# Seven block products instead of eight for the second half of batch 6, with the two-batch products two tiles sooner

## Chip, cores and metric

The kernel runs on one core of a Trainium2 chip. The metric is the device time of one execution in microseconds (us). Before the change the median of three runs is 302.89 us (302.75 to 303.0).

The engines are called as in the profile: PE is TensorE's matmuls, PEld its weight loads, DVE VectorE, ACT ScalarE, POOL GpSimd, SP SyncE. ACT, POOL and SP also issue DMAs.

## What is computed

There are 8 batches of 1024 tokens with 512 features, all in float32. Each batch has its own 512 x 512 matrix, made from the batch's condition vector:

```python
# cond: layernorm, two dense layers with an exact GELU -> x_a, x_b, each [8, 512, 8]
layer = base_layer[None] + einsum('bdr,bkr->bdk', x_a, x_b)
x = x + (x + einsum('btc,bco->bto', x, layer))          # first layer and residuals
ys = cond / sqrt(512)
d = rsqrt(einsum('bi,io->bo', ys * ys, weight * weight) + 1e-8)
out = x + einsum('bsi,io->bso', x * ys[:, None, :], weight) * d[:, None, :]
```

Both layers and all residual additions are linear in x. So for each batch `out[b] = x[b] @ M[b]` with `M[b] = (2 I + layer) (I + diag(ys) weight diag(d))`.

## The kernel before, in words

The matrices `M[b]` are made on the chip (tiles `q`), and then x is multiplied by them. Float32 values are split for PE into a rounded part and the rest, both of the type float32r. A product a r is taken as three matmuls: high by high, high by low, low by high.

The work on x is the main loop. `main(b, t)` computes 128 tokens by 512 outputs: 4 chunks of the contraction by three matmuls of 128x512, 12 in all, into one bank of PSUM (pool `po`, four banks). ACT copies it to SBUF and issues the store. `load_x` loads half a batch (SP), and `split_x` splits 256 tokens of it (a cast on ACT, a subtract on DVE). `split_p` splits `q[b]` into `ph[b]` and `pl[b]`. The lists in `after` say which other steps are emitted behind which tile; `place(i)` turns the running number i of a tile into batch and tile.

The matrices of batches 4 and 5, and of 6 and 7, are made two at a time by `Pair`, with seven block products for each pair of batches. One `unit` of it (six matmuls of 128x512, 14 units in all) is emitted behind each tile from the number `first` on. `early` and `prepare` make its right-hand sides on DVE and ACT, and `rank_term` adds the rank-8 part (four matmuls, four adds on DVE).

Batch 7 is not done by `main`. `Seven` multiplies it with Strassen's scheme in Winograd's form: the batch's x and the matrix are cut into 2 x 2 blocks, and seven block products take the place of eight. `make_right` forms four sums of blocks of `q[7]` on DVE, casts them on ACT and subtracts on DVE for the rest; it also splits the three blocks that are used as they are. `make_left(g)` does the same with sums of blocks of x, for a quarter of the tokens of each half of the batch. `part(g)` then runs the seven products. Each is 12 matmuls of 128x256, 6 for each of two groups of 128 tokens. They go in the order 1, 5, 6, 2, 7, 3, 4 into three banks: `w` takes products 1, 6, 7 and 4, each added onto the one before it, `z` takes 5 and 3, and `v` takes 2. After each product the bank is copied by ACT (1, 5, 6, 4) or added by DVE (2, 7, 3) into the output tiles `o1` and `o2`. So a product of bank w has to wait until the evacuation of the one before it has read the bank. `part` stores `o1` behind product 3 and `o2` behind product 4. In the last part product 4 is copied and stored for each 128 tokens by itself, out of one bank.

Matmuls keep the order of the program text. On DVE and ACT the steps of the main loop and of `Seven` are not held to it: the compiler that lays out the program fixes the order, and then each engine works its queue in order. Tiles of a tag share as many buffers as `bufs` says. `late_pools` closes the pools from which the matrices were made, and the tiles of `Seven` (`tl`, `th`, `sums`, `sl`, `sh`, `x22`, `o2`) then use their memory. `q`, the loaded x, `xs` and `xa` are in pool `big`, nine buffers.

Of the kernel before, what the change touches and what calls it, by code (L numbers as in the profile page):

```python
# [30 lines left out]
def cond_resid_kernel(ctx: ExitStack, tc: tile.TileContext, small, cond, condrows, consts,  # L31
# [12 lines left out]
    def mm(*args, **kw):  # L44
        tc.keep_in_program_order(nc.tensor.matmul(*args, **kw))  # L45
# [601 lines left out]
    def p_tiles(b):  # L647
        ph[b] = ppool.tile([P, KC, D], F32R, tag="ph", name=f"ph_{b}")
        pl[b] = ppool.tile([P, KC, D], F32R, tag="pl", name=f"pl_{b}")
# [173 lines left out]
    class Seven:  # L823
# [5 lines left out]

        ORDER = (1, 5, 6, 2, 7, 3, 4)

        def __init__(self, b):
            self.b, self.left = b, {}

        def make_right(self):
            b, late = self.b, pools["late"]
            t = late.tile([P, 4, 2, HD], F32R, tag="tl", name=f"tl_{b}", bufs=1)  # L840
            h = late.tile([P, 4, 2, HD], F32R, tag="th", name=f"th_{b}", bufs=1)
            raws = late.tile([P, 4, 2, HD], F32, tag="sums", name=f"traw_{b}", bufs=2)
            t1, t2, t3, t4 = (raws[:, i] for i in range(4))
            b11, b12 = q[b][:, 0:2, 0:HD], q[b][:, 0:2, HD:D]
            b21, b22 = q[b][:, 2:4, 0:HD], q[b][:, 2:4, HD:D]
            p_tiles(b)
            for rows, cols in ((slice(0, 4), slice(0, HD)), (slice(2, 4), slice(HD, D))):
                nc.scalar.copy(ph[b][:, rows, cols], q[b][:, rows, cols])
                nc.vector.tensor_sub(pl[b][:, rows, cols], q[b][:, rows, cols],
                                     ph[b][:, rows, cols].bitcast(F32))  # L850
            for o, x, y in ((t1, b12, b11), (t2, b22, t1), (t3, b22, b12), (t4, b21, t2)):
                nc.vector.tensor_sub(o, x, y)
            for i in range(0, 4, 2):
                at = slice(i, i + 2)
                nc.scalar.copy(h[:, at], raws[:, at])
                nc.vector.tensor_sub(t[:, at], raws[:, at], h[:, at].bitcast(F32))
            self.right = {5: (h[:, 0], t[:, 0]), 6: (h[:, 1], t[:, 1]), 7: (h[:, 2], t[:, 2]),
                          4: (h[:, 3], t[:, 3])}
            for p, rows, cols in ((1, slice(0, 2), slice(0, HD)), (2, slice(2, 4), slice(0, HD)),
                                  (3, slice(2, 4), slice(HD, D))):  # L860
                self.right[p] = ph[b][:, rows, cols], pl[b][:, rows, cols]

        def make_left(self, g):
            b, late = self.b, pools["late"]
            at = slice(2 * P * g, 2 * P * (g + 1))
            top, low = raw[b, 0][:, :, at], raw[b, 1][:, :, at]
            a11, a12, a21, a22 = top[:, 0:2], top[:, 2:4], low[:, 0:2], low[:, 2:4]
            s = late.tile([P, 4, 2, 2 * P], F32R, tag="sl", name=f"sl_{b}_{g}", bufs=2)
            h = late.tile([P, 4, 2, 2 * P], F32R, tag="sh", name=f"sh_{b}_{g}", bufs=2)
            x = late.tile([P, 2, 2, 2 * P], F32R, tag="x22", name=f"x22_{b}_{g}", bufs=2)  # L870
            xa = big.tile([P, 2, KC, 2 * P], F32R, tag="big", name=f"xa_{b}_{g}")
            nc.scalar.copy(xa[:, 0], top)
            nc.vector.tensor_sub(xa[:, 1], top, xa[:, 0].bitcast(F32))
            raws = late.tile([P, 4, 2, 2 * P], F32, tag="sums", name=f"sraw_{b}_{g}", bufs=2)
            s1, s2, s3, s4 = (raws[:, i] for i in range(4))
            nc.vector.tensor_add(s1, a21, a22)
            nc.vector.tensor_sub(s2, s1, a11)
            for i, (o, u, v) in enumerate(((s3, a11, a21), (s4, a12, s2))):
                nc.vector.tensor_sub(o, u, v)
            for i in range(0, 4, 2):  # L880
                two = slice(i, i + 2)
                nc.scalar.copy(h[:, two], raws[:, two])
                nc.vector.tensor_sub(s[:, two], raws[:, two], h[:, two].bitcast(F32))
            nc.scalar.copy(x[:, 0], a22)
            nc.vector.tensor_sub(x[:, 1], a22, x[:, 0].bitcast(F32))
            self.left[g] = {5: (h[:, 0], s[:, 0]), 6: (h[:, 1], s[:, 1]), 7: (h[:, 2], s[:, 2]),
                            3: (h[:, 3], s[:, 3]), 4: (x[:, 0], x[:, 1]),
                            1: (xa[:, 0, 0:2], xa[:, 1, 0:2]), 2: (xa[:, 0, 2:4], xa[:, 1, 2:4])}

        def product(self, g, p, bank, m, first):  # L890
            (lh, ll), (rh, rl) = self.left[g][p], self.right[p]
            for kk in range(2):
                for i, (a, r) in enumerate(((lh, rh), (lh, rl), (ll, rh))):
                    mm(bank[:, m, :], a[:, kk, m * P:(m + 1) * P], r[:, kk, :],
                       start=(first and m == 0 and kk == 0 and i == 0),
                       stop=(kk == 1 and i == 2), skip_group_check=True)

        def part(self, g, last):
            b, bank = self.b, {}
            o1, o2 = (pools["late"].tile([P, 2, D], F32, tag="o2", name=f"o{i}_{b}_{g}", bufs=3)  # L900
                      for i in range(2))
            for p in self.ORDER:
                key = {5: "z", 3: "z", 2: "v"}.get(p, "w")
                first = p in (1, 5, 2)
                if first:
                    pool, tag = (acc, "acc") if key == "v" else (po, "po")
                    bank[key] = pool.tile([P, 2, HD], F32, tag=tag, name=f"s{key}_{b}_{g}")
                u = bank[key]
                for m in range(2):
                    self.product(g, p, u, m, first)  # L910
                    if p == 4 and last:
                        nc.scalar.copy(o2[:, m, 0:HD], u[:, m])
                        self.store(o2, g, 1, slice(m, m + 1))
                if p == 1:
                    nc.scalar.copy(o1[:, :, 0:HD], u)
                elif p == 5:
                    nc.scalar.copy(o2[:, :, HD:D], u)
                elif p == 6:
                    nc.scalar.copy(o1[:, :, HD:D], u)
                elif p == 2:  # L920
                    nc.vector.tensor_add(o1[:, :, 0:HD], u, o1[:, :, 0:HD])
                elif p == 7:
                    nc.vector.tensor_add(o2[:, :, HD:D], u, o2[:, :, HD:D])
                elif p == 3:
                    nc.vector.tensor_add(o1[:, :, HD:D], u, o1[:, :, HD:D])
                    self.store(o1, g, 0, slice(0, 2))
                elif not last:
                    nc.scalar.copy(o2[:, :, 0:HD], u)
                    self.store(o2, g, 1, slice(0, 2))

        def store(self, o, g, half, ms):
            at = half * HT + 2 * P * g
            nc.scalar.dma_start(
                out[self.b, at + P * ms.start:at + P * ms.stop, :].rearrange("(m p) d -> p m d", p=P),
                o[:, ms, :])
# [16 lines left out]
    place = lambda i: divmod(i, NTT)  # L952
    for b in range(1, 4):
        first = (b - 1) * NTT
        at(*place(max(0, 4 * b - 8)), load_rank, b)
        at(*place(4 * b - 2), rank_term, b)
        for j in range(2):
            at(*place(first + 3 + j), split_p, b, j)
    for b, first in ((4, 13), (6, 30)):

        at(*place(first - 9), load_d, b)
        at(*place(first - 6), new_pair, b)
# [9 lines left out]
        at(*place(first + 15), split_p, b, 0)  # L972
        at(*place(first + 16), split_p, b, 1)
        if b == 4:
            at(*place(first + 19), split_p, b + 1, 0)
            at(*place(first + 21), split_p, b + 1, 1)
    seven = Seven(NB - 1)
    at(*place(46), late_pools)
    at(*place(47), seven.make_right)
    at(*place(49), load_x, NB - 1, 0)  # L980
    at(*place(50), load_x, NB - 1, 1)
    at(*place(52), seven.make_left, 0)
    at(*place(54), seven.make_left, 1)

    for b in range(NB - 1):
        for t in range(NTT):
            if t == 0 and b + 2 < NB:
                p_tiles(b + 1)
            main(b, t)
            i = b * NTT + t  # L990
            if t % 4 == 0 and i + 4 < (NB - 1) * NTT:
                load_x(*divmod(i // 4 + 1, NHALF))
            if t % 2 == 0 and i + 4 < (NB - 1) * NTT:
                split_x(*divmod(i // 2 + 2, NTT // 2))
            for f, args in after.get((b, t), ()):
                f(*args)
    for g in range(2):
        seven.part(g, g == 1)


# [67 lines left out]
```

## Time and profile before

| | us |
|---|---|
| median of three runs | 302.89 |
| the profiled execution's own time | 302.81 |
| its span, from the first to the last instruction | 301.0 |
| PE busy | 294.3 |
| DVE busy | 194.0 |
| ACT busy | 150.2 |

The granted clock of TensorE is 1.000 as the mean of the span. The first 80 us make the matrices of batches 0 to 3. From 80.7 on the main loop runs, and from 276.5 on the two parts of batch 7. The profile comes from one execution. "Busy" is time in which at least one instruction of the engine ran. Matmuls overlap one another, so the distance of their starts tells their price, not their duration. In a timeline a bracket gives the idle time of the engine before the instruction and what ended it. The chain of waits goes back from the last instruction to what released each one.

### The profile page before, as it was taken

The page shows a single profiled execution, that of the slowest core. Times are in us where ns is not written, and L with a number is a line of the kernel's source. Part 1 is how long each engine was busy: PE and PEld are TensorE (multiplying, and loading weights), DVE is VectorE, ACT ScalarE, POOL GpSimd, SP SyncE. Part 2 cuts the span into 40 slices and gives each one's busy share as a digit, 9 for nine tenths or more (in the row PEclk, how much of TensorE's full clock was granted, in tenths as well). Part 3 has the DMA queues.
Part 4 walks back from the last instruction along what each step waited for, and adds up shares of the span by engine and source line. Part 5 has one row for each costly group of instructions (what it writes and reads, how often), then busy time and mean ns, then how long its engine had stood idle before and what let it go on. Part 6 is the DMA issues. An engine that isn't in the chain of part 4 may idle for free.

```text
span 301.0 us, 3809 instructions
## 1 busy us (share of the span) xinstructions
PE 294.3 (98%) x1429; PEld 224.8 (75%) x1429; DVE 194.0 (64%) x287; ACT 150.2 (50%) x218; POOL 34.8 (12%) x74
## 2 busy tenths in 40 slices
PE   7999999999999999999999999999999999999994
PEld 2655465466878778888888877888888877888993
DVE  4779750979569889794157549994356238994201
ACT  4756132256566672572457535664465436855130
POOL 0011000057104505100000018000000000000000
PEclk9999999999999999999999999999999999999999
DMA  6999999696519888186124347725144364432033
GB/s 207 412 426 418 407 423 416 216 327 182 197 70 312 320 250 273 72 244 210 69 89 193 87 192 188 233 82 199 50 194 152 128 209 140 165 117 93 12 143 139
DMA packets 19027, 62.12 MB, mean 206 GB/s; under 512 B 2736, under 2 KB 2992, under 8 KB 14656
## 3 DMA queue, kind: packets, MB, share of 16 engines
q1 hardware_dynamic: 6064, 38.78, 34.6%
q10 hardware_dynamic: 9168, 16.78, 15.0%
q0 software_dynamic: 3776, 6.31, 7.7%
q8 instruction: 11, 0.18, 0.2%
q14 instruction: 8, 0.07, 0.1%
HBM read 44.02 MB, written 17.84 MB: 206 GB/s over the span
## 4 chain that ended last, share of the span: by engine, by line
PE 86%; DMA 5%; DVE 5%; ACT 2%; issue 1%; SPq 0%; ACTq 0%
PE po L45 51%; PE pp L45 13%; PE pq L45 7%; PE sw L45 4%; DMA w<-in_w 4%; PE px L45 3%; PE pg L45 2%; PE sz L45 2%; DVE n L62 2%; DMA b_raw<-in_baseT 2%; PE pr L45 1%; PE sv L45 1%; PE pt_t L45 1%; ACT work L62 1%; DVE scr L62 0%
## 5 line engine op out<-in xcount | busy, mean ns | idle before, releaser
L45 PE MATMUL po<-ph,xs 128*128 128x512 f32 x448 | 144.9, 391 | 0.0
L45 PEld LDWEIGHTS po<-ph,xs 128*128 128x128 f32 x448 | 84.1, 188 | 19.3 <-issue 1.7
L45 PE MATMUL po<-pl,xs 128*128 128x512 f32 x224 | 87.3, 390 | 0.0
L62 ACT COPY o<-po 128x512 f32<-128x512 f32 x56 | 32.8, 586 | 60.8 <-PE po L45 60.8
L45 PEld LDWEIGHTS po<-pl,xs 128*128 128x128 f32 x224 | 42.1, 188 | 8.6
L62 DVE TENSOR_TENSOR xs<-x,xs 128x1024 fp32r<-128x1024 f32 x28 | 34.0, 1220 | 10.5 <-ACT xs L62 10.5
L62 DVE TENSOR_TENSOR nl_p<-n,nh_p 128x1024 fp32r<-128x1024 f32 x14 | 17.1, 1222 | 23.1 <-ACT nh_p L62 23.0
L62 ACT CAST xs<-x 128x1024 fp32r<-128x1024 f32 x28 | 29.1, 1052 | 1.2 <-DMA x<-in_x 1.0
L62 DVE TENSOR_TENSOR q<-pr,q 128x512 f32<-128x512 f32 x32 | 20.1, 684 | 13.6 <-PE pr L45 13.6
L511 POOL DMA_DIRECT2D fa<-kept_a x28 | 13.7, 506 | 77.9 <-PE pr L45 77.2
L45 PE MATMUL pq<-nh,bh 128*128 128x512 f32 x48 | 19.8, 412 | 0.0
L45 PE MATMUL pq<-nl,bh 128*128 128x512 f32 x48 | 19.1, 398 | 0.1
L62 ACT COPY q<-pp 128x512 f32<-128x512 f32 x20 | 11.7, 587 | 14.9 <-PE pp L45 14.1
L45 PE MATMUL pq<-nh,bl 128*128 128x512 f32 x48 | 18.9, 394 | 0.0
L62 DVE SCALAR_TENSOR_TENSOR n<-w_sb,ysT,d 128x512 f32<-128x512 f32 x24 | 17.7, 746 | 1.5 <-DMA d<-d_out 1.5
L62 DVE TENSOR_TENSOR pl<-q,ph 128x1024 fp32r<-128x1024 f32 x14 | 16.9, 1220 | 0.1
L62 ACT CAST nh_p<-n 128x1024 fp32r<-128x1024 f32 x14 | 14.7, 1052 | 3.5 <-DVE n L62 1.9
L62 ACT CAST ph<-q 128x1024 fp32r<-128x1024 f32 x14 | 14.6, 1053 | 3.4 <-DVE q L62 3.1
L45 PE MATMUL px<-w,hT 128*32 128x512 f32 x128 | 16.0, 601 | 0.1
L45 PEld LDWEIGHTS pq<-nh,bh 128*128 128x128 f32 x48 | 9.0, 188 | 8.4 <-issue 5.0
L511 POOL DMA_DIRECT2D ft<-kept_t x28 | 13.8, 512 | 4.9 <-DMA kept_t<-st_t 4.9
L62 ACT CAST nh<-n 128x512 fp32r<-128x512 f32 (+1 forms) x10 | 6.9, 707 | 11.5 <-DVE n L62 11.5
(193 smaller groups left out, 407.1 us busy)
## 6 DMA issues: line engine op xcount, KB each, us to landing
w<-in_w SPq DMA_DIRECT2D x16, 1024.0 KB, 10.7
x<-in_x SPq DMA_DIRECT2D x16, 1024.0 KB, 5.3
out<-o ACTq DMA_DIRECT2D x58, 256.0 KB, 2.1
ft<-kept_t POOLq DMA_DIRECT2D x28, 64.0 KB, 3.4
fa<-kept_a POOLq DMA_DIRECT2D x28, 64.0 KB, 3.2
d<-d_out POOLq DMA_DIRECT2D x6, 256.0 KB, 3.9
out<-o ACTq DMA_DIRECT2D x3, 512.0 KB, 2.9
w_sb<-in_weight SPq DMA_DIRECT2D x2, 512.0 KB, 5.3
```

Source lines behind the costliest of these rows:

```text
L45: tc.keep_in_program_order(nc.tensor.matmul(*args, **kw))
L62: return lambda *a, **kw: pin(f(*a, **kw)) if InOrder.on else f(*a, **kw)
L511: nc.gpsimd.dma_start(fold[name, b][32 * c:32 * c + 32, :], kept[name, g][32 * i:32 * i + 32, :])
```

## The change

- `Seven` now takes a batch by halves: part g has the g-th 512 tokens, `make_left(g)` the sums of that half.
- The second half of batch 6 is done by `Seven` too. The main loop ends after 52 tiles instead of 56, and three parts follow: batch 6's second half, then batch 7's two halves. `make_left(1)` of batch 7 is emitted between the first two of these.
- For batch 6 `make_right` has `whole` true and leaves out the split, since `ph[6]` and `pl[6]` exist already. `tl` and `th` get two buffers, `sums` one instead of two.
- Both pairs start two tiles sooner, with their rank terms; the rank terms of batches 2 and 3 move up too, the split of batch 5 goes one tile later, and `late_pools` moves from behind tile 46 to behind tile 44.
- Bank w moves from pool `po` to `acc`. In the last part it is two banks, one for each 128 tokens; each of its evacuations is then two narrower ones, and product 4 runs through before it is copied in the text.

```diff
-        def make_right(self):
+        def make_right(self, whole):
             b, late = self.b, pools["late"]
-            t = late.tile([P, 4, 2, HD], F32R, tag="tl", name=f"tl_{b}", bufs=1)
-            h = late.tile([P, 4, 2, HD], F32R, tag="th", name=f"th_{b}", bufs=1)
-            raws = late.tile([P, 4, 2, HD], F32, tag="sums", name=f"traw_{b}", bufs=2)
+            t = late.tile([P, 4, 2, HD], F32R, tag="tl", name=f"tl_{b}", bufs=2)
+            h = late.tile([P, 4, 2, HD], F32R, tag="th", name=f"th_{b}", bufs=2)
+            raws = late.tile([P, 4, 2, HD], F32, tag="sums", name=f"traw_{b}", bufs=1)
...
-            p_tiles(b)
             for rows, cols in ((slice(0, 4), slice(0, HD)), (slice(2, 4), slice(HD, D))):
+                if whole:
+                    break
                 nc.scalar.copy(ph[b][:, rows, cols], q[b][:, rows, cols])
...
         def make_left(self, g):
             b, late = self.b, pools["late"]
-            at = slice(2 * P * g, 2 * P * (g + 1))
-            top, low = raw[b, 0][:, :, at], raw[b, 1][:, :, at]
+            top, low = (raw[b, g][:, :, 2 * P * i:2 * P * (i + 1)] for i in range(2))
...
-            raws = late.tile([P, 4, 2, 2 * P], F32, tag="sums", name=f"sraw_{b}_{g}", bufs=2)
+            raws = late.tile([P, 4, 2, 2 * P], F32, tag="sums", name=f"sraw_{b}_{g}", bufs=1)
...
-        def product(self, g, p, bank, m, first):
+        def product(self, g, p, banks, first):
             (lh, ll), (rh, rl) = self.left[g][p], self.right[p]
-            for kk in range(2):
-                for i, (a, r) in enumerate(((lh, rh), (lh, rl), (ll, rh))):
-                    mm(bank[:, m, :], a[:, kk, m * P:(m + 1) * P], r[:, kk, :],
...
+            for m in range(2):
+                bank, at = (banks[0], m) if len(banks) == 1 else (banks[m], 0)
+                for kk in range(2):
+                    for i, (a, r) in enumerate(((lh, rh), (lh, rl), (ll, rh))):
+                        mm(bank[:, at, :], a[:, kk, m * P:(m + 1) * P], r[:, kk, :],
...
                 if first:
-                    pool, tag = (acc, "acc") if key == "v" else (po, "po")
-                    bank[key] = pool.tile([P, 2, HD], F32, tag=tag, name=f"s{key}_{b}_{g}")
...
+                    pool, tag = (po, "po") if key == "z" else (acc, "acc")
+                    bank[key] = [pool.tile([P, 2, HD], F32, tag=tag, name=f"s{key}{i}_{b}_{g}")
+                                 for i in range(2 if key == "w" and last else 1)]
+                self.product(g, p, bank[key], first)
+                o, cols = {1: (o1, slice(0, HD)), 2: (o1, slice(0, HD)), 3: (o1, slice(HD, D)),
+                           6: (o1, slice(HD, D)), 4: (o2, slice(0, HD)), 5: (o2, slice(HD, D)),
+                           7: (o2, slice(HD, D))}[p]
+                for m, u in enumerate(bank[key]):
+                    u, to = (u, slice(0, 2)) if len(bank[key]) == 1 else (u[:, 0:1], slice(m, m + 1))
+                    if p in (2, 3, 7):
+                        nc.vector.tensor_add(o[:, to, cols], u, o[:, to, cols])
+                    else:
+                        nc.scalar.copy(o[:, to, cols], u)
+                    if p in (3, 4):
+                        self.store(o, g, int(p == 4), to)
...
-        at(*place(max(0, 4 * b - 8)), load_rank, b)
-        at(*place(4 * b - 2), rank_term, b)
+        at(*place(max(0, 3 * b - 7)), load_rank, b)
+        at(*place(3 * b - 1), rank_term, b)
...
-    for b, first in ((4, 13), (6, 30)):
+    for b, first in ((4, 11), (6, 28)):
...
-            at(*place(first + 19), split_p, b + 1, 0)
-            at(*place(first + 21), split_p, b + 1, 1)
-    seven = Seven(NB - 1)
-    at(*place(46), late_pools)
-    at(*place(47), seven.make_right)
-    at(*place(49), load_x, NB - 1, 0)
-    at(*place(50), load_x, NB - 1, 1)
-    at(*place(52), seven.make_left, 0)
-    at(*place(54), seven.make_left, 1)
+            at(*place(33), split_p, b + 1, 0)
+            at(*place(35), split_p, b + 1, 1)
+    sevens = [Seven(NB - 2), Seven(NB - 1)]
+    at(*place(44), late_pools)
+    at(*place(45), sevens[0].make_right, True)
+    at(*place(46), load_x, NB - 2, 1)
+    at(*place(48), sevens[0].make_left, 1)
+    at(*place(48), sevens[1].make_right, False)
     at(*place(49), load_x, NB - 1, 0)
+    at(*place(51), sevens[1].make_left, 0)
+    at(*place(51), load_x, NB - 1, 1)
...
+    HALF = NTT // 2
+    TILES = (NB - 1) * NTT - HALF
+    for i in range(TILES):
...
-    for g in range(2):
-        seven.part(g, g == 1)
+    sevens[0].part(1)
+    sevens[1].make_left(1)
+    sevens[1].part(0)
+    sevens[1].part(1, True)
```

More of the change, by code (lines that the diff above doesn't have):

```diff
@@ L888, in make_left, with part @@
                             1: (xa[:, 0, 0:2], xa[:, 1, 0:2]), 2: (xa[:, 0, 2:4], xa[:, 1, 2:4])}
-        def product(self, g, p, bank, m, first):
+        def product(self, g, p, banks, first):
             (lh, ll), (rh, rl) = self.left[g][p], self.right[p]
-            for kk in range(2):
-                for i, (a, r) in enumerate(((lh, rh), (lh, rl), (ll, rh))):
-                    mm(bank[:, m, :], a[:, kk, m * P:(m + 1) * P], r[:, kk, :],
-                       start=(first and m == 0 and kk == 0 and i == 0),
-                       stop=(kk == 1 and i == 2), skip_group_check=True)
-        def part(self, g, last):
+            for m in range(2):
[3 more added lines that the diff above has]
+                        mm(bank[:, at, :], a[:, kk, m * P:(m + 1) * P], r[:, kk, :],
+                           start=(first and at == 0 and kk == 0 and i == 0),
+                           stop=(kk == 1 and i == 2), skip_group_check=True)
+        def part(self, g, last=False):
             b, bank = self.b, {}
@@ L905, in part @@
                 if first:
-                    pool, tag = (acc, "acc") if key == "v" else (po, "po")
-                    bank[key] = pool.tile([P, 2, HD], F32, tag=tag, name=f"s{key}_{b}_{g}")
[L908 to L929, printed above, removed]
@@ L931, in store @@
+                for m, u in enumerate(bank[key]):
[6 more added lines that the diff above has]
+                        self.store(o, g, int(p == 4), to)
         def store(self, o, g, half, ms):
-            at = half * HT + 2 * P * g
+            at = g * HT + 2 * P * half
@@ L974, in cond_resid_kernel @@
         if b == 4:
-            at(*place(first + 19), split_p, b + 1, 0)
-            at(*place(first + 21), split_p, b + 1, 1)
-    seven = Seven(NB - 1)
-    at(*place(46), late_pools)
-    at(*place(47), seven.make_right)
-    at(*place(49), load_x, NB - 1, 0)
-    at(*place(50), load_x, NB - 1, 1)
-    at(*place(52), seven.make_left, 0)
-    at(*place(54), seven.make_left, 1)
[L985 to L996, printed above, removed]
-    for g in range(2):
-        seven.part(g, g == 1)
+            at(*place(33), split_p, b + 1, 0)
[6 more added lines that the diff above has]
+    at(*place(48), sevens[1].make_right, False)
+    at(*place(49), load_x, NB - 1, 0)
+    at(*place(51), sevens[1].make_left, 0)
[3 more added lines that the diff above has]
+    for i in range(TILES):
+        b, t = divmod(i, NTT)
+        if t == 0:
+            p_tiles(b + 1)
+        main(b, t)
+        if t % 4 == 0 and i + 4 < TILES:
+            load_x(*divmod(i // 4 + 1, NHALF))
+        if t % 2 == 0 and i + 4 < TILES:
+            split_x(*divmod(i // 2 + 2, NTT // 2))
+        for f, args in after.get((b, t), ()):
+            f(*args)
+    sevens[0].part(1)
+    sevens[1].make_left(1)
+    sevens[1].part(0)
+    sevens[1].part(1, True)
 def kernel(**inputs):
```

## The prediction

> **What bounds the kernel now.** First the page. It says that TensorE (PE) works nearly the whole span, while VectorE (DVE) and ScalarE (ACT) fill up in places.
>
> ```profile
> span 301.0 us, 3809 instructions
> PE 294.3 (98%) x1429; PEld 224.8 (75%) x1429; DVE 194.0 (64%) x287; ACT 150.2 (50%) x218; POOL 34.8 (12%) x74
> ...
> DVE  4779750979569889794157549994356238994201
> ```
>
> One slice is 7.5 us: DVE is full from 245 to 275. Then the chain of waits in order of time, which gives PE's prices. Columns: start, duration, what.
>
> ```profile
> 249.04 27.47 PE po L45 x120
> 276.51 1.43 PE sw L45 x12
> 277.94 1.44 PE sz L45 x12
> ...
> 293.78 1.46 PE sz L45 x12
> 295.26 0.70 DVE o L925
> 296.40 0.99 PE sw L45 x6
> ```
>
> Ten tiles of batch 6 take 27.47. Less the 0.23 by which the first tile after a rank term is longer (2.95 at 245.66 beside 2.72 everywhere), a tile is 2.724 us. A product is 1.44, a part of seven 10.08 (276.51 to 286.59). PE has no hole from 75 us to 295.24; the only one after that is ahead of the last six matmuls. So removed PE work counts in full, and so does each new PE wait. Now the timeline of DVE (start, duration, engine, line, operation, idle before):
>
> ```profile
> 255.10 1.23 DVE L873 TENSOR_TENSOR xa<-x,xa 128x1024 fp32r<-128x1024 f32 x1 [1.11 <-ACT xa L872]
> 256.24 0.69 DVE L852 TENSOR_TENSOR traw<-q 128x512 f32<-128x512 f32 x1
> ...
> 273.53 1.23 DVE L883 TENSOR_TENSOR sl<-sraw,sh 128x1024 fp32r<-128x1024 f32 x1 [0.21 <-ACT sh L882]
> 282.37 0.69 DVE L921 TENSOR_TENSOR o<-sv,o 128x512 f32<-128x512 f32 x1 [7.62 <-PE sv L45]
> ```
>
> One make_right and two make_lefts fill DVE from 255.10 to 274.76 and end before the parts begin: nothing disputes the evacuations. ACT shows what happens when something does:
>
> ```profile
> 260.51 1.05 ACT L855 CAST th<-traw 128x1024 fp32r<-128x1024 f32 x1 [0.15 <-DVE traw L852]
> 261.46 0.58 ACT L62 COPY o<-po 128x512 f32<-128x512 f32 x1
> ...
> 277.98 0.59 ACT L915 COPY o<-sw 128x512 f32<-128x512 f32 x1 [0.85 <-PE sw L45]
> ```
>
> The copy at 261.46 is tile 49's, done on PE at 260.17: a cast that stands earlier in the program text went ahead, and it came 1.3 late. Tile 53's (271.06) came 0.9 late. Four po banks hid that. In a part there is no spare bank. Last, the stretches of the tail (PE, PEld, DVE, ACT, POOL busy, clock, DMA share, GB/s):
>
> ```profile
> 296.80:297.00 0.20, 0.20 (x4) 0.20 (x4) 0.00 (x0) 0.00 (x0) 0.00 (x0) 1.00 0.53 205
> 297.00:297.20 0.20, 0.20 (x4) 0.18 (x2) 0.00 (x0) 0.00 (x0) 0.00 (x0) 1.00 0.96 369
> ...
> 299.40:299.60 0.20, 0.00 (x0) 0.00 (x0) 0.00 (x0) 0.00 (x0) 0.00 (x0) 1.00 0.97 369
> 299.60:299.80 0.20, 0.00 (x0) 0.00 (x0) 0.00 (x0) 0.00 (x0) 0.00 (x0) 1.00 0.22 72
> ```
>
> The last 1.05 MB leave at full DMA share from 296.85 to 299.62.
>
> **The part, on PE.** Four tiles go, 4 x 2.724 = 10.90; a part of 10.08 comes: -0.82. Weight loads rise from 48 to 84. They start every 0.12 us in the parts, 0.19 long each, beside the matmuls, and are in the 1.44. The Trainium skill (TensorE: Matmul & The Clock Gate, "The mechanism" and "LDWEIGHTS") speaks against this: a load of 128 columns takes about 107 ns and overlaps a running matmul only in another row group. By that, as an estimate, 36 more loads would cost 3.9 us and the part would lose 3.0; the rows show the overlap and decide.
>
> **The last bank in two.** PE's last six matmuls no longer wait for the first copy: PE ends 1.1 sooner after the last sz product. But the tail begins with the store of o1, issued at 295.99, 0.03 after the add of the sixth product (295.26 to 295.95), and that stays. From there 1.05 MB at full share set the end; the last store, issued at 297.82, was still behind them. Gain 0 (at most the 0.7 by which PE and ACT let the last store go sooner). The narrower copies (0.37 for 0.59) lie in ACT's gaps of 0.85.
>
> **The pairs two tiles sooner.** Batch 4's first product moves from 120.91 to about 115.4; its right half was done at 112.15. Ahead of it in the text come one more rank term (four adds, 2.4); two pl subtracts (2.3) and one xs (1.1) fall behind it. So it stays near 112: 3 us of cover. Later products have about 8 (the subtract of 128.28 ends at 129.5, its product starts at 137.41). Batch 6's pair moves with its rank terms by the same two tiles. POOL: rank loads still follow rank term 1 (89.7), land in 3.4 and are wanted at about 106; SP: batch 6's second half had landed by 235, long before 252. Cost 0; with the cover gone, about 1.2 for one late subtract.
>
> **The preparation, where the price lies.** DVE starts a 512-wide operation every 0.60 and a 1024-wide one every 1.14 (256 to 274). Needed: make_right of batch 6, 4 x 0.60 + 2 x 1.14 = 4.7; make_left(6,1) 5.3, its xa done earlier, where xs stood at 236.11; make_right of batch 7, 1.14 + 0.60 + 4.7 = 6.4; make_left(7,0) 5.3 + 1.14 = 6.4. Sum 22.8. Two splits of batch 6's x go, but one had been done at 236. The start is set by the memory of the late pool: after the change tile 44 is the last before it, and ends at 251.99 - 5.45 = 246.5; copy 0.1 + 0.6, store landing 2.1: 249.3. (Before, the same sum gives 254.8, and the first sum ran at 256.24.) So DVE is through at 249.3 + 22.8 = 272.1 at the earliest. xa of (7,1) slips in (1.14), and with one buffer for the sums instead of two each block waits for its own casts; I take 0.3 for each of four: 274.4.
>
> The part of batch 6 begins at 276.51 - 10.90 = 265.6. Its w bank holds products 1, 6, 7 and 4, so each waits for the evacuation of the one before it:
> - Product 6 waits for ACT's copy of product 1: 1.44 less 0.65 leaves 0.8. th casts of batch 7 stand ahead; one is covered, two are not. Between 0 and 1.3; I take 0.2, as two of nine tile copies exceeded 0.8, by 0.5 and 0.1.
> - Product 4 waits for DVE's add of product 7, ready at 265.6 + 7.2 = 272.8, due by 274.2. The add of product 2 stands before it. With DVE through at 274.4 it ends at 275.7 if both stand behind, 1.5 late, and at 275.1 if the first found a hole. Between 0 (DVE through by 272.9) and 1.9 (another 0.4 of idle time); I take 0.9.
> - Product 6 of (7,0) waits for ACT's copy of product 1. make_left(7,1) stands before that part in the text, and its sh casts wait for the sl/sh buffer that product 3 of batch 6 frees. With the two waits above that part begins at 276.8. On ACT then stand the last copy of batch 6's part 0.59, x22 cast 0.62, store 0.34, two casts 2.1, so to 280.5; the copy ends at 281.1, product 6 is due at 276.8 + 2.88 = 279.7, 1.4 sooner. Between 0 and 1.5; I take 0.9, as some of the casts may find an earlier place.
> Behind each such wait the whole of PE is queued. Nothing here can give time back: PE has no other work in the text to fill with.
>
> **Sum.** The profiled execution took 302.81 (span 301.0 and 1.8 around it; median of the runs 302.89). 302.81 - 0.82 + 0.2 + 0.9 + 0.9 = 303.99, say 304.0.
>
> **Rivals.** (a) Faster: the evacuations are in time. Decided by DVE being through with make_left(7,0) before 272.9; the earliest is 272.1, so it takes nearly no idle time, or adds placed between two blocks. For it: before, 19.3 us of such work took 19.7. Against: one sums buffer, and a start that was later than my sum before. 302.81 - 0.82 = 302.0; chance 0.25, with waits up to 0.3. (b) One of the three waits only, 0.3 to 1.5 in all: about 302.9; chance 0.17. (c) The split bank does shorten the end: another -0.7, so 301.3 with no waits; the DMA stretches speak against, 0.04, inside (a). (d) The earlier pairs stall once or twice, +1.2 each: 0.06, inside the slower case.
>
> **Chances and range.** Forecast (waits of 1.5 and more) 0.58. About 0.2%, 0.6 us, is what a measurement of this kernel can tell: faster under 302.3, slower over 303.5. The forecast's own range, 303.5 to 305.2 (waits of 3.2). Eight in ten: from 301.9, which takes in (a), to 305.2.
>
> **What would show it.** PE rows: four tiles fewer and three parts with a gap ahead of "sw" product 6 or 4; in the waits, PE for ACT or DVE o in the parts. DVE without a hole from 249 to past 274. The last stores' stretch at full share, 2.8 long, from about 0.9 after o1's issue. Wrong if the three parts stand at 10.08 each; if PE waits at the start of a part or ahead of a pp product; or if the end comes sooner after the last sz product than 5.8 (295.24 to 301.0).

## The result: slower by 0.8%, because the new part waits three times

The changed kernel takes 305.36 us, median of six runs (305.17 to 305.47), beside 302.88 for the kernel before in the same session (302.74 to 303.0). The ratio is 1.0082, 95% interval 1.0069 to 1.0095. The profiled execution took 305.17 with a span of 303.4; before, 302.81 and 301.0. So 2.4 of the 2.5 us can be looked for in the traces.

First the page of the changed kernel: span, instructions, busy times, and DVE in forty slices.

```profile
span 303.4 us, 3915 instructions
PE 294.9 (97%) x1465; PEld 226.5 (75%) x1465; DVE 205.1 (68%) x303; ACT 153.2 (50%) x224; POOL 34.8 (11%) x74
DVE  4779840979569999872564399941572469999411
```

PE has 36 matmuls more, as many as the change adds. DVE has 11.1 us more work, and its full stretch now reaches slice 37, which is 273 to 281: it runs into the parts, which begin at 265.46. Two windows of the changed kernel, then the same two of the kernel before (columns: stretch, length, then busy time of PE, PEld, DVE, ACT and POOL with the number of instructions, clock, DMA share, GB/s):

```profile
245.00:265.00 20.00, 20.00 (x89) 16.54 (x89) 17.45 (x24) 12.32 (x17) 0.00 (x0) 1.00 0.54 203
265.00:285.00 20.00, 17.81 (x142) 17.11 (x141) 17.06 (x22) 10.80 (x15) 0.00 (x0) 1.00 0.19 70
```

```profile
245.00:265.00 20.00, 20.00 (x91) 15.80 (x91) 18.20 (x24) 14.02 (x18) 0.00 (x0) 1.00 0.43 160
265.00:285.00 20.00, 20.00 (x124) 18.03 (x123) 10.92 (x14) 8.10 (x13) 0.00 (x0) 1.00 0.20 76
```

Before, DVE's work of 265 to 285 was 10.9 and PE stood still nowhere. Now it is 17.1, and PE stands still for 2.19 at a clock of 1.00 throughout. The waits of PE from 260 on, summed up (line that waited, what it waited for, total, times, longest):

```profile
PE sw L45 <- ACT o L920: 1.3, 2, 0.9
PE sw L45 <- DVE o L918: 0.9, 1, 0.9
```

L920 is the copy and L918 the add that empty a bank. There are no other waits of PE in the whole stretch from 75 us to the end. In PE's timeline the three are these; the bracket is the idle time just before and its releaser:

```profile
268.94 0.39 PE L45 MATMUL sw<-th,sh 128*128 128x256 f32 x1 [0.44 <-ACT o L920]
269.16 0.28 PE L45 MATMUL sw<-tl,sh 128*128 128x256 f32 x1
269.28 0.28 PE L45 MATMUL sw<-th,sl 128*128 128x256 f32 x1
...
275.84 0.39 PE L45 MATMUL sw<-th,x 128*128 128x256 f32 x1 [0.89 <-DVE o L918]
...
281.27 0.39 PE L45 MATMUL sw<-th,sh 128*128 128x256 f32 x1 [0.86 <-ACT o L920]
```

The brackets are too small to be the price: they count from the end of the matmul before, which is listed 0.28 long although matmuls start 0.12 apart. The price is read from starts. Product 6 of batch 6's part was due two products after the first, at 265.46 + 2.88 = 268.34, and began at 268.94: 0.60 late. Its first two matmuls then start 0.22 apart instead of 0.12, so the product takes 1.53 instead of 1.44. That is 0.69 for the first wait. In the same way the second (product 4 of that part) costs 1.05 + 0.09 = 1.14, and the third (product 6 of batch 7's first part) 1.02 + 0.10 = 1.12. The three parts take 11.91, 11.20 and 10.08 by their starts: the last one has no wait.

The chain of waits in order of time shows what the chain before did not: from 249.3 to 281.3 it runs on DVE and ACT alone (start, duration, what):

```profile
243.63 5.68 PE po L45 x24
...
254.15 2.27 DVE tl L856 x2
...
267.35 1.06 ACT th L855
...
272.91 2.27 DVE sl L882 x2
275.18 1.20 DVE o L918 x2
...
280.12 0.61 ACT x L883
280.74 0.49 ACT o L920
281.22 0.04 issue
281.27 1.70 PE sw L45 x12
```

Every late evacuation (o) has a step of the preparation directly ahead of it on the same engine. Now DVE's timeline; before, nothing of the preparation was left when the parts began:

```profile
249.92 1.29 DVE L852 TENSOR_TENSOR traw<-q 128x512 f32<-128x512 f32 x2 [2.52 <-ACT o L62]
...
265.29 1.22 DVE L872 TENSOR_TENSOR xa<-x,xa 128x1024 fp32r<-128x1024 f32 x1
266.42 0.68 DVE L852 TENSOR_TENSOR traw<-q,traw 128x512 f32<-128x512 f32 x1
...
272.23 0.68 DVE L918 TENSOR_TENSOR o<-sv,o 128x512 f32<-128x512 f32 x1
272.83 2.35 DVE L882 TENSOR_TENSOR sl<-sraw,sh 128x1024 fp32r<-128x1024 f32 x2
275.10 0.68 DVE L918 TENSOR_TENSOR o<-sw,o 128x512 f32<-128x512 f32 x1
```

and ACT's (ACTq is the issue of a DMA):

```profile
265.41 1.05 ACT L855 CAST th<-traw 128x1024 fp32r<-128x1024 f32 x1 [1.83 <-DVE traw L852]
266.36 0.58 ACT L62 COPY o<-po 128x512 f32<-128x512 f32 x1
266.97 0.34 ACTq L821 DMA_DIRECT2D out<-o  x1
267.35 1.05 ACT L855 CAST th<-traw 128x1024 fp32r<-128x1024 f32 x1 [0.41 <-DVE traw L852]
268.31 0.58 ACT L920 COPY o<-sw 128x512 f32<-128x512 f32 x1
...
278.22 1.06 ACT L881 CAST sh<-sraw 128x1024 fp32r<-128x1024 f32 x1
278.22 0.38 ACTq L926 DMA_DIRECT2D out<-o  x1
279.17 1.05 ACT L881 CAST sh<-sraw 128x1024 fp32r<-128x1024 f32 x1
280.12 0.61 ACT L883 CAST x<-x 128x512 fp32r<-128x512 f32 x1
280.64 0.58 ACT L920 COPY o<-sw 128x512 f32<-128x512 f32 x1
```

Wait 1: the copy of product 1 could have begun at about 267.1 (before, such a copy began 1.63 after the first matmul of its product), but it began at 268.31, behind a th cast. That cast of 267.35 had its sum ready at 267.10 (266.42 and 0.68); what it stood behind was the copy of the last tile and the issue of its store. These again stood behind another th cast, which had waited for DVE until 265.41. Wait 2: product 7 was done at about 273.5, but its add began at 275.10, behind two sl subtracts. Wait 3: the copy of 280.64 stands behind two sh casts and an x22 cast.

At the end of the span the last transfers fill the DMA engines as before (columns as in the windows above):

```profile
299.00:299.20 0.20, 0.00 (x0) 0.00 (x0) 0.00 (x0) 0.05 (x1) 0.00 (x0) 1.00 0.37 143
299.20:299.40 0.20, 0.00 (x0) 0.00 (x0) 0.00 (x0) 0.20 (x1) 0.00 (x0) 1.00 1.04 399
...
301.60:301.80 0.20, 0.00 (x0) 0.00 (x0) 0.00 (x0) 0.00 (x0) 0.00 (x0) 1.00 1.00 379
301.80:302.00 0.20, 0.00 (x0) 0.00 (x0) 0.00 (x0) 0.00 (x0) 0.00 (x0) 1.00 0.30 103
```

1.05 MB leave from about 299.13 to 301.86, 2.7 long; before it was 2.8. From the last sz product's end to the end of the span it is 6.0 now (297.38 to 303.4), 5.8 before.

### The profile page after: what moved, and what is told of

The parts are those of the page before. It is cut to its first block, busy times and chain, and to the rows that moved or that the text cites. A ratio compares the mean times of both kernels' runs of the same rounds, so it can differ in the third digit from the quotient of the medians.

```text
span 303.4 us, 3915 instructions
## 1 busy us (share of the span) xinstructions
PE 294.9 (97%) x1465; PEld 226.5 (75%) x1465; DVE 205.1 (68%) x303; ACT 153.2 (50%) x224; POOL 34.8 (11%) x74
## 4 chain that ended last, share of the span: by engine, by line
PE 81%; DVE 13%; ACT 3%; issue 2%; ACTq 0%
PE po L45 42%; PE pp L45 13%; PE pq L45 9%; PE px L45 4%; PE sw L45 3%; PE warm L45 2%; PE pg L45 2%; DVE n L62 2%; DVE sl L882 1%; PE sz L45 1%; DVE traw L852 1%; PE pr L45 1%; DVE tl L856 1%; PE sv L45 1%; DVE o L918 1%
## 5 line engine op out<-in xcount | busy, mean ns | idle before, releaser
L45 PE MATMUL po<-ph,xs 128*128 128x512 f32 x416 | 135.1, 392 | 0.0
L45 PEld LDWEIGHTS po<-ph,xs 128*128 128x128 f32 x416 | 78.1, 188 | 18.0 <-issue 1.7
L45 PE MATMUL po<-pl,xs 128*128 128x512 f32 x208 | 81.1, 390 | 0.0
L62 ACT COPY o<-po 128x512 f32<-128x512 f32 x52 | 30.5, 586 | 57.9 <-PE po L45 57.9
L45 PEld LDWEIGHTS po<-pl,xs 128*128 128x128 f32 x208 | 39.1, 188 | 8.0
L62 DVE TENSOR_TENSOR xs<-x,xs 128x1024 fp32r<-128x1024 f32 x26 | 31.5, 1220 | 7.5 <-ACT xs L62 7.5
L62 DVE TENSOR_TENSOR nl_p<-n,nh_p 128x1024 fp32r<-128x1024 f32 x14 | 17.1, 1224 | 20.3 <-ACT nh_p L62 20.3
L62 ACT CAST xs<-x 128x1024 fp32r<-128x1024 f32 x26 | 27.1, 1052 | 0.9 <-DVE xs L62 0.5
L920 ACT COPY o<-sw 128x512 f32<-128x512 f32 (+1 forms) x12 | 5.7, 478 | 18.0 <-PE sw L45 9.1
```

What stands on the lines that cost most here:

```text
L62: return lambda *a, **kw: pin(f(*a, **kw)) if InOrder.on else f(*a, **kw)
L920: nc.scalar.copy(o[:, to, cols], u)
```

## Experiments

The theory is the queue: in the parts bank w needs each evacuation in time, and ACT and DVE, which work in order, have preparation of batch 7 standing ahead. Three others would put the time elsewhere: in the new bank arrangement of the last part, in the pairs' earlier products, or in the memory (one sums buffer, and what had to shrink for it). A fifth, that the part itself is dearer than 10.08, is excluded by the last part, which took 10.08. Each ratio is against the kernel before on the same chip, whose medians were 302.88 to 303.01. "Product 6 (6,1)" is product 6 of batch 6's second half. The waits come from one profiled execution of each kernel; in the row "two sums, all of batch 7's preparation after the part" (304.40) and in the last row (306.60) that was the slowest of its executions.

| kernel | median, us | ratio, 95% interval | waits left in the parts (idle before the matmul) |
|---|---|---|---|
| the change | 305.36 | 1.0082 [1.0069, 1.0095] | 0.44, 0.89, 0.86 |
| only the last bank in two | 302.82 | 1.0001 [0.9988, 1.0014] | none |
| only the pairs sooner | 303.11 | 1.0003 [0.9995, 1.0012] | 0.46, ahead of the last six matmuls, as before |
| batch 7's sums of x left out | 303.04 | 1.0005 [0.9996, 1.0014] | 0.68 |
| and its sums of q too | 302.37 | 0.9977 [0.9967, 0.9987] | none |
| make_left(7,1) after the part | 304.19 | 1.0043 [1.003, 1.0055] | 0.77, 0.88 |
| both make_left of 7 after the part | 303.64 | 1.0023 [1.0011, 1.0035] | 0.33, 0.22 |
| the same with four output tiles | 303.38 | 1.0013 [1.0004, 1.0022] | 0.33, 0.18 |
| two sums buffers | 304.95 | 1.0066 [1.0054, 1.0079] | 0.80, 1.14 |
| the room for that alone | 305.45 | 1.0082 [1.0068, 1.0096] | 0.61, 0.90, 0.85 |
| two sums, all of batch 7's preparation after the part | 303.61 | 1.0025 [1.0014, 1.0036] | 0.51, 0.52 |
| subtracts of batch 7's x on POOL | 309.89 | 1.0237 [1.0221, 1.0253] | 3.79, 0.84, 0.85 |
| the same, lefts after, four output tiles | 309.18 | 1.0196 [1.0179, 1.0212] | 4.08 |
| late_pools one tile sooner | 304.83 | 1.0055 [1.0042, 1.0068] | 0.99, 1.09 |
| that, lefts after, four output tiles | 305.05 | 1.0073 [1.0055, 1.0092] | 1.08, 1.10 |

### The other parts of the change, each alone

In the kernel before, only the last bank in two (bank w in pool `acc`, the evacuations by 128 tokens):

```diff
-                    pool, tag = (acc, "acc") if key == "v" else (po, "po")
-                    bank[key] = pool.tile([P, 2, HD], F32, tag=tag, name=f"s{key}_{b}_{g}")
+                    pool, tag = (po, "po") if key == "z" else (acc, "acc")
+                    bank[key] = [pool.tile([P, 2, HD], F32, tag=tag, name=f"s{key}{i}_{b}_{g}")
+                                 for i in range(2 if key == "w" and last else 1)]
```

> The kernel before with bank w in the other pool and the last one in two banks, nothing else. If the tail is set by the 1.05 MB behind the store of o1 at full DMA share: no change, 302.7 to 303.1. If the 0.22 us by which the tail grew in the changed kernel comes from the two banks: 303.1. Rival (c) of the prediction, that PE's earlier end shortens the tail: 302.2.

It measured 1.0001 [0.9988, 1.0014]. PE no longer waits ahead of the last six matmuls, and nothing comes of it: in its chain the last sz product ends at 295.08 and the span at 300.9, 5.8 later as before. What follows the add is the transfers.

And only the pairs two tiles sooner, with their rank terms and the split of batch 5:

```diff
-        at(*place(max(0, 4 * b - 8)), load_rank, b)
-        at(*place(4 * b - 2), rank_term, b)
+        at(*place(max(0, 3 * b - 7)), load_rank, b)
+        at(*place(3 * b - 1), rank_term, b)
...
-    for b, first in ((4, 13), (6, 30)):
+    for b, first in ((4, 11), (6, 28)):
```

> The kernel before with both pairs two tiles sooner and the rank terms and the split of batch 5 moved as in the change; batch 7's parts and the late pool as before. Theory Q: PE keeps its row without a hole, 302.7 to 303.1. Rival (d): one or two late subtracts of a pair, 304.1 or more.

It measured 1.0003 [0.9995, 1.0012], with no wait of PE from 75 to 290 us. Two of the rivals are gone: what is lost, is lost by the part and its preparation.

### Less work ahead of the evacuations

Batch 7's two make_left use the sums of batch 6's second half:

```diff
+            if b == NB - 1:
+                s, h = sevens[0].left[1][0]
+            else:
+                s, h = self.sums(late, g, a11, a12, a21, a22)
```

> Leaves out, for both halves of batch 7, the four sums of x with their casts and subtracts (4.7 us of DVE and 2.1 us of ACT for each half); products 5, 6, 7 and 3 of batch 7 read batch 6's sums instead. All matmuls, evacuations, loads and stores stay. Theory Q (the evacuations of bank w stand behind preparation in the queues of ACT and DVE): with 9.4 us of preparation gone the three waits of 0.69, 1.14 and 1.11 us go, every part takes 10.08 us on PE, and the time is 302.88 - 0.82 + 0.2 = about 302.2. Rival R (three parts in a row, bank w in another pool or the halves of a batch cost the time by themselves): the waits stay, 304.5 or more.

Waits 2 and 3 are gone, and 303.04 is a miss: wait 1 is there, longer than in the change.

```profile
269.46 0.39 PE L45 MATMUL sw<-th,sh 128*128 128x256 f32 x1 [0.68 <-ACT o L928]
```

ACT's timeline in this kernel says why: the th cast, which this experiment leaves in, still stands ahead of the copy.

```profile
267.87 1.05 ACT L855 CAST th<-traw 128x1024 fp32r<-128x1024 f32 x1 [0.41 <-DVE traw L852]
268.83 0.58 ACT L928 COPY o<-sw 128x512 f32<-128x512 f32 x1
```

So the next run left out the th of batch 7 as well:

```diff
+            if whole:
+                t, h = self.right_sums(late)
+            else:
+                t, h = sevens[0].th
```

> The kernel of e1, which leaves out the sums of x of batch 7, and make_right's sums, casts and subtracts for batch 7 left out too (products 5, 6, 7 and 4 of batch 7 read batch 6's right-hand sums). Matmuls, evacuations, loads and stores stay. The first wait, which stayed in e1, was on casts of make_right, so now there is none: each part 10.08 us, and the time gives the part's price alone with the tail: 302.88 - 0.82 + 0.2 = 302.2. If a wait or 0.5 us more is left, the 0.82 was not there.

302.37 is close to the 302.2 that was expected: 0.9977 [0.9967, 0.9987]. PE waits nowhere in the parts; they begin at 265.82 in the chain, and the last sz product ends at 294.63, 28.81 later, which is twenty products of 1.44. With nothing in its way the part on PE is worth what the prediction says; and all three waits vanish with work on DVE and ACT, though PE's work is the same.

### The same work, in another order

`make_left(7,1)` behind the first part of batch 7 instead of ahead of it:

```diff
-    sevens[1].make_left(1)
     sevens[1].part(0)
+    sevens[1].make_left(1)
```

> The changed kernel with one call moved: make_left(1) of batch 7 is emitted behind part(0) of batch 7 instead of ahead of it, so that part's evacuations go ahead of it in the text. Theory Q: the third wait (1.02 + 0.09 us ahead of product 6 of part (7,0)) goes, the first two stay at 0.69 and 1.14; 305.36 - 1.1 = about 304.3. If the left sums then come late, part (7,1) starts late by up to 1 us and the gain is lost. Rival R: 305.4.

304.19, as expected. The third wait is gone and the first two are still there:

```profile
269.04 0.39 PE L45 MATMUL sw<-th,sh 128*128 128x256 f32 x1 [0.77 <-ACT o L920]
...
275.94 0.39 PE L45 MATMUL sw<-th,x 128*128 128x256 f32 x1 [0.88 <-DVE o L918]
```

Then both make_left of batch 7, each behind the part ahead of it in the text:

```diff
-    at(*place(51), sevens[1].make_left, 0)
...
-    sevens[1].make_left(1)
+    sevens[1].make_left(0)
     sevens[1].part(0)
+    sevens[1].make_left(1)
```

> The changed kernel with both make_lefts of batch 7 emitted behind the part ahead of them (make_left(0) behind part(1) of batch 6, make_left(1) behind part(0) of batch 7): every evacuation of a part now stands ahead of them in the text. All work stays. Theory Q: the second wait (1.14 us, product 4 of (6,1) on DVE's add) falls to 0.3 or less and the third (1.11) goes; the first (0.69, the copy of product 1 behind casts of make_right, which was not moved) stays between 0.4 and 0.9. 305.36 - 1.0 - 1.1 = 303.3. Rival R: 304.3 or more. If the left sums are late instead, PE waits at product 5 of (7,0) or (7,1).

303.64 [1.0011, 1.0035]: 0.3 above what was expected, and 1.7 below the change with not one instruction less. Wait 1 went too: the last of DVE's sums for th now starts at 265.58 instead of 266.42, and its cast at 266.30 instead of 267.35. DVE's timeline at the place of wait 2:

```profile
272.84 1.21 DVE L882 TENSOR_TENSOR sl<-sraw,sh 128x1024 fp32r<-128x1024 f32 x1
273.98 0.68 DVE L918 TENSOR_TENSOR o<-sw,o 128x512 f32<-128x512 f32 x1
274.58 1.21 DVE L882 TENSOR_TENSOR sl<-sraw,sh 128x1024 fp32r<-128x1024 f32 x1
```

The add of product 7 now stands between the two subtracts, at 273.98 instead of 275.10. DVE still does all of that work, and the second subtract ends no sooner than in the change (275.79, 275.18). That shows the mechanism most directly: the place in the queue counts. What stays are 0.33 there and 0.22 ahead of product 7 (7,0), whose bank is held by the copy of product 6, behind two sh casts.

A fourth output tile, paid for by one buffer less of the main loop's outputs, was tried on top, since an output tile seemed to hold back a copy:

```diff
-            o1, o2 = (pools["late"].tile([P, 2, D], F32, tag="o2", name=f"o{i}_{b}_{g}", bufs=3)
+            o1, o2 = (pools["late"].tile([P, 2, D], F32, tag="o2", name=f"o{i}_{b}_{g}", bufs=4)
...
-        pools["o"] = ctx.enter_context(tc.tile_pool(name="opool2", bufs=4))
+        pools["o"] = ctx.enter_context(tc.tile_pool(name="opool2", bufs=3))
```

> The kernel of e5 with four output tiles in the parts instead of three (three instead of four in the main loop's last ones), nothing else. In e5 ACT's copy of product 5 of (7,0) stood 0.9 us for an output tile whose store had not landed, and with it the casts and the copy of product 1's successors behind it. If that was the 0.5 us that product 6 of (7,0) lost, it goes: about 0.4 below e5 on the same chip, 303.0 to 303.2; if not, 303.6 as e5.

303.38 [1.0004, 1.0022], 0.2 above the expectation. The waits are 0.33 and 0.18, so the tile was not the reason. Its median is the lowest of the versions that do the whole work, and it is still not faster than the kernel before: by the starts, its first two parts take 0.65 and 0.44 longer than 10.08, together more than the 0.82 that a part saves.

### Two sums buffers

One sums buffer makes each block wait for its own casts. Two of them, and the room for it taken from `o2` and the main loop's outputs:

```diff
-            raws = late.tile([P, 4, 2, HD], F32, tag="sums", name=f"traw_{b}", bufs=1)
+            raws = late.tile([P, 4, 2, HD], F32, tag="sums", name=f"traw_{b}", bufs=2)
...
-            raws = late.tile([P, 4, 2, 2 * P], F32, tag="sums", name=f"sraw_{b}_{g}", bufs=1)
+            raws = late.tile([P, 4, 2, 2 * P], F32, tag="sums", name=f"sraw_{b}_{g}", bufs=2)
```

> The changed kernel with two buffers for the sums again; to make room the output tiles of the parts have two instead of three and the main loop's last ones three instead of four. Theory Q with the single buffer as the cause of DVE's late end: DVE is through with make_left(7,0) 1.5 us or more sooner (273.5 or earlier instead of 275.1), the first wait goes, the second falls below 0.3, the third stays between 0 and 1.1: 302.6 to 303.6. If DVE's sum of work alone sets the end, the waits stay: 305.0 or more.

304.95: a miss by more than 1 us. DVE is through with make_left(7,0) 1.35 sooner, at 273.75, and waits 1 and 2 are gone. But the casts, no longer held back, come in front of another copy:

```profile
269.25 1.05 ACT L881 CAST sh<-sraw 128x1024 fp32r<-128x1024 f32 x1 [0.26 <-DVE sraw L876]
270.45 1.05 ACT L881 CAST sh<-sraw 128x1024 fp32r<-128x1024 f32 x1 [0.15 <-DVE sraw L878]
271.40 0.58 ACT L920 COPY o<-sw 128x512 f32<-128x512 f32 x1
```

The copy of product 6 stands behind two of them, and PE waits 0.80 ahead of product 7 at 272.03. Wait 3 is still there, now 1.14 long. Preparation that is done sooner is of no use if it stands ahead of an evacuation.

> The changed kernel with only the room made for e7: two output tiles instead of three in the parts, three instead of four in the main loop's last ones, sums with one buffer. Control for e7. All theories: 305.4, within 0.3; above it if the output tiles bind.

The room alone (two `o2`, three outputs, still one sums buffer) measured 305.45, no different from the change and with the same three waits, so the smaller pools cost nothing. The single sums buffer does have a share in waits 1 and 2; but with two of them other waits take their place, and the time falls by just 0.5, from 305.45 to 304.95. Both ideas together, two sums buffers and all of batch 7's preparation behind the part:

> Two buffers for the sums as in e7, and all preparation of batch 7 (make_right and both make_lefts) emitted behind the part ahead of it. Theory Q: at most one wait of up to 0.5 us is left; 302.88 - 0.82 + 0.2 + 0 to 0.5 = 302.3 to 302.8, the first version not slower than the kernel before. Rival R: 303.5 or more.

303.61, above the expectation, with two waits of 0.5, ahead of products 7 and 4 (6,1).

### Relief by POOL, and an earlier start

To shorten DVE's queue without changing its order, the subtracts for xa and x22 of batch 7 went to POOL, first in the change as it is:

```diff
-            nc.vector.tensor_sub(xa[:, 1], top, xa[:, 0].bitcast(F32))
+            by = nc.gpsimd if b == NB - 1 else nc.vector
+            by.tensor_sub(xa[:, 1], top, xa[:, 0].bitcast(F32))
```

> The changed kernel, order as it is, with only the subtracts of xa and x22 of batch 7 on POOL: 3.5 us less on DVE, nothing else moved or left out. If DVE's sum of work sets the second wait (product 4 of (6,1) on the add of product 7), DVE is through by 272.9 and that wait (1.14) goes; the first (0.69) shrinks, as make_right's last sum no longer stands behind xa; the third (1.11) shrinks to 0.5 or less: 302.8 to 303.8. If order alone does it, the adds stay behind the left sums and the time stays at 305.0 or more.

309.89: worse by 4.5 than the change. The same with both lefts behind their parts and four output tiles:

> Nothing left out. The kernel of e5 (both make_lefts of batch 7 behind the part ahead of them), the subtracts of xa and x22 of batch 7 on POOL instead of DVE (3.5 us of DVE work ahead of part (7,1) go), and four output tiles in the parts instead of three (in e5 an evacuation waited for a store's landing). Theory Q: no wait above 0.3 us, 302.88 - 0.82 + 0.2 + 0.3 at most: 302.2 to 302.6. Rival P: POOL's subtracts are slow or hold up DVE, and PE waits at the start of part (7,0) or (7,1): 303.5 or more.

309.18. DVE was not relieved but stopped. Timelines of POOL and of DVE in the first of the two kernels:

```profile
251.48 2.63 POOL L873 TENSOR_TENSOR xa<-x,xa 128x1024 fp32r<-128x1024 f32 x1 [69.92 <-ACT xa L871]
...
265.38 2.69 POOL L873 TENSOR_TENSOR xa<-x,xa 128x1024 fp32r<-128x1024 f32 x1 [6.60 <-ACT xa L871]
```

```profile
251.76 2.90 DVE L885 TENSOR_TENSOR x<-x,x 128x512 fp32r<-128x512 f32 x1
...
265.13 3.49 DVE L852 TENSOR_TENSOR traw<-q 128x512 f32<-128x512 f32 x2
```

An operation that takes 0.69 elsewhere took 2.90, and a pair that takes 1.29 took 3.49. Each ended 0.55 after POOL's subtract did. The th casts then waited for these sums, the copy of product 1 for the casts, and PE 3.79 for the copy.

Not all of the 4.5 is this wait. Before it the granted clock was 1.00; from 272 to 275 it was 0.50. Product 6, which began at 272.27, took 2.73, where product 6 of the change took 1.53 behind its short wait: 1.2 us for the lower clock. In the second kernel, after the wait of 4.08, the clock was 0.50 from 274 to 276 as well. None of the waits near 1 us is followed by that: in the change the clock is 1.00 behind all three.

The last attempt: if `late_pools` comes one tile sooner, DVE should start sooner.

```diff
-    at(*place(44), late_pools)
+    at(*place(43), late_pools)
```

> The changed kernel with the late pool opened behind tile 43 instead of 44, one tile sooner; no step leaves its place in the text. Theory Q: the 2.5 us in which DVE stood idle before its first sum at 249.9 go, DVE is through with make_left(7,0) about 2 us sooner (273 instead of 275.1), so the second wait (1.14) falls to 0.3 or less and the third (1.11) to 0.6 or less; the first (0.69) may stay. 302.88 - 0.82 + 0.2 + 0.4 to 1.6 = 302.7 to 303.9, middle 303.3. If the order in the text alone does it, the waits stay: 305.0 or more.

304.83, and the start did not move:

```profile
249.81 1.30 DVE L852 TENSOR_TENSOR traw<-q 128x512 f32<-128x512 f32 x2 [2.15 <-DMA out<-o]
```

It was 249.92 in the change. The waits changed places once more. With the reordered lefts and four output tiles it was no better:

> The kernel of e11 (both make_lefts of batch 7 behind the part ahead of them, four output tiles) with the late pool opened one tile sooner. Theory Q: at most one wait of 0.5 us is left: 302.3 to 302.8, faster than or even with the kernel before. If it stays at 303.4 as e11, the start of the preparation is not what binds there.

305.05. Neither run says anything on how much of wait 2 the amount of work would account for, because the start, which they were to change, stayed.

## Why the prediction was wrong in size and right in kind

**The part, -0.82: right.** The last part takes 10.08, and with the preparation left out all three do. The 36 more weight loads lie within that price: it is 84 matmuls at 0.12. The first part began 10.89 sooner than before (265.46 and 276.35 by the first matmuls), as the four tiles of 10.90 say.

**The last bank and the pairs, 0 each: right,** each by its own run.

**The three waits, 0.2 + 0.9 + 0.9 = 2.0: this is the step that failed.** The mechanism was right: they are at the three products that were named, on the engines that were named. Their sizes were not: they cost 0.69 + 1.14 + 1.12 = 2.95, with three terms too small and one that was left out:

- Wait 1 was put at 0.2 between bounds of 0 and 1.3, from how often tile copies had been late before. That was a frequency from another stage. ACT's queue gives it: behind the last tile's copy and store a whole th cast stood ahead of the copy of product 1, which came 1.2 late. The cover was 0.6, not the 0.8 that the prediction took: before, such a copy began 1.63 after the first matmul of its product, 0.2 after the product's 1.44, and the 0.2 was left out.
- Waits 2 and 3 were put at 0.9 each, middle values, because adds and casts might find an earlier place. One did, product 2's add (272.23). Product 7's did not, and three casts stood ahead of wait 3's copy.
- The prediction's arithmetic for the worst order gave DVE's add ending at 275.7 and ACT's copy at 281.1, and they ended at 275.78 and 281.22. That they came so near is partly luck. The worst order for the add had product 2's add behind the preparation too; it was not, but DVE was through with make_left(7,0) at 275.1 instead of 274.4, of which 0.6 is its later start. Part (7,0) began at 277.37 instead of 276.8, but ACT's steps up to the copy's end took 3.85 from there instead of 4.3: the issue of the store, which the prediction put in line with them, ran beside a cast.
- Each wait costs 0.09 or 0.10 more than the lateness of its first matmul, as the second one starts 0.22 behind it instead of 0.12. No term stood for it; three times, 0.28.

**The tail, 0: off by 0.2.** Of it 0.08 lies between the last sz product and the store's issue (0.83 instead of 0.75), and about 0.16 behind the last transfer (301.86 to 303.4; before, 299.62 to 301.0). The bank in two is not the reason, since that kernel alone has 5.8, nor are the waits, since the kernel without batch 7's preparation has 6.0 (294.63 to 300.6). What is, stays open.

**The sum.** -0.82 + 2.95 + 0.2 = 2.33 explains the spans, 303.4 less 301.0; 0.1 more is how the profiled executions stand to their medians. The forecast's own range ended at waits of 3.2 with nothing for the tail, which is 305.2: the profiled execution, 305.17, lies at its edge and the median, 305.36, beyond it.

**The rivals.** That the evacuations are in time needed DVE through by 272.9; it was 275.1. The split bank's 0.7 did not come (1.0001 [0.9988, 1.0014]), nor a stall of the pairs (1.0003 [0.9995, 1.0012]).

**What would have shown it.** All three signs came: three parts, the first two with gaps ahead of product 6 or 4, DVE without a hole above 0.2 from 249.9 to past 275, and the last stores' stretch 2.7 long, 0.9 after the issue of 298.21. Open is also what the amount of DVE's work does by itself apart from its order: the runs that were to shorten it on POOL stopped it instead.

## What to carry to other kernels

When matmuls accumulate in one bank through evacuations, the work that other engines do for the next stage has to be placed between those evacuations by hand: follow each in-order queue instruction by instruction, and do not take the middle of its bounds for the end that this gives. A saving of 0.8 on the busiest engine is no gain if the preparation that it asks for moves into a stretch where that engine has nothing to fill a wait with. Taking one item out of such a queue can shift the rest in front of another evacuation, so count the waits of the whole stretch after each edit.

## What the hardware showed beyond that

- A subtract on POOL holds up DVE. POOL's subtract of 128x1024 took 2.63 where DVE needs 1.22, its 128x512 took 1.30 where DVE needs 0.69, and a DVE operation that had begun beside it ended only 0.55 after it. The Trainium skill says as much: a VectorE instruction with two SBUF inputs contends with a GpSimd instruction that reads SBUF, and the shared port pair is "an exclusive lock" (SBUF — State Buffer, "Who interferes with whom"); two-input elementwise work is about twice as slow on GpSimd (GPSIMD Engine Reference, "4.1 Engine selection"). The rows agree with both: a stop until POOL was done, and 2.2 and 1.9 times.
- After a wait of PE, the first two 128x256 matmuls start 0.22 apart instead of 0.12, at each of the three waits. So a short wait costs a tenth of a microsecond more than the lateness of its first matmul.
- After PE's two waits of about 4 us (3.79 and 4.08) the granted clock was 0.50 for some 3 us, and 128x256 matmuls started 0.21 apart. After waits of about 1 us it stayed at 1.00.
